# A graph network with soft and routed experts on one core: earlier expert weights, a token list made on chip, more logit tiles and smaller pieces of work in the edge stage

## The chip, the cores and the metric

The kernel runs on one core of a Trainium2 chip. Its engines are TensorE (PE; PEld is the loading of its weights), VectorE (DVE), ScalarE (ACT), GpSimd (POOL) and SyncE (SP, which issues transfers); ACT and POOL issue transfers too. Each engine works through its own instructions in order and waits at semaphores for the others. The metric is the time of one execution on the device in microseconds, the median of several.

## The reference

The input is x (1250 rows of 768 numbers) and 40000 edges from a source row to a destination row, sorted by destination. Four blocks follow each other, each of the form x = x + f(layernorm(x)):

```
# 1. two layers of graph attention (8 heads of 96, then 1 head of 768); in each:
fs, fd = x @ Ws + bs, x @ Wd + bd
e      = leaky_relu(fs[src] + fd[dst], 0.2)
logit  = (e * attn).sum(per head)                  # one per edge
alpha  = softmax of logit over the edges with the same dst
out    = elu(sum over those edges of alpha * fs[src])      # then a layer norm with weights
# 2. soft experts: 32 experts with 32 slots each (1024 slots), hidden width 192
logits = l2norm(x) @ (scale * l2norm(phi))
slots  = softmax(logits over an expert's slots).T @ l2norm(x)
eo     = gelu(slots @ w1[e] + b1[e]) @ w2[e] + b2[e]
out    = softmax(logits over all 1024 slots) @ eo
# 3. two graph convolutions with self-loops and symmetric normalization
# 4. routed experts: 8 experts, hidden width 1152, the top 2 of 8 for each row
out    = sum of gate * (gelu(x @ w1[e] + b1[e]) @ w2[e] + b2[e])
```

## The kernel before

The 1250 rows are ten blocks of 128 partitions (NB = 10; the last has 98 rows). The edges are sorted on the chip into 100 buckets (NBK), by block of the destination (i) and block of the source (j), k = 10 i + j; a bucket has up to 512 edges (CAP), four columns of 128. The stages run one after the other, each fed by the one before. Four of them bear on the change.

**The second edge stage** (`edge_logits`, L361 to L585; heads = 1) makes one logit for each edge. For every bucket k of a loop, and every column q, PE sums the source's and the destination's features by products with one-hot matrices into `z` (L425; each operand in a high and a low half, 8 matmuls for a column), DVE takes the positive part times the attention vector and adds it up into column q of the tile `lg` (L440), and ACT copies the linear part (L447). Two buckets' worth of steps later DVE adds the linear part (L458), and POOL scatters each column, 128 single numbers, into a table in DRAM, one entry for each pair of rows (L463). `done` holds the newest bucket first, and q's scatter belongs to `done[1 + 2 q]`: column 0 of a bucket is scattered two iterations after its sums, column 3 eight iterations after. `lg` has 12 buffers in this stage and 8 in the first edge stage. A second use of the same loop, with heads = 8, is the first edge stage.

At the end of the loop (k = 99, 100 and 101) `dense.join` (L707; its addition is L714) adds the two halves of the linear features of five, four and one of the ten blocks into `rows`. Three pairs of tables (`lt`, logits, and `ct`, edge counts) for the blocks 0 to 2 are loaded during the loop.

**The second dense stage** (`run_alone`, L774) takes one destination block at a time, in an order that is written out for PE, DVE, ACT and POOL. `maxima` is the negated maximum of a block's logits, `exponentials` its exp (L798), `turn` transposes the exp on PE (L807) and multiplies it by the counts on DVE (L808), `product` multiplies by the features (L813). Each product of block b is followed by a generator `ending` (L1130), of which `go_on` runs one step at each call, two calls for each block: elu, layer norm, the row sum on POOL (L1148 to L1150), the second norm and the squares (ACT), until `xn` holds the normalized rows. Its remaining steps run in the soft stage's loop, with the same `go_on`. `phi_norm` normalizes phi between the products. `neg`, a helper of elu and the square's output, has one buffer, g has three; the layer norm's weights `lw`, `lb` are loaded into tiles of their own at the start, and `phi` too, in SP's queue.

**The soft experts** (L1267 to L1342): the slots' inputs `slT` are a product over all rows (L1267). Then eight groups of four experts. `first_layer(g)` loads four w1 (on SP's queue) and four w2 (on ACT's), 576 KB each, with eight buffers each, multiplies (L1298; b1 is added by a product at the start) and applies gelu (ACT, L1301). `second_layer` follows with w2, and `combine` with the 1250 rows (L1327); the sum of group g runs after the second layer of g+1. The pool `route`, with xn and g, is closed after `slT`; then the pool `experts` opens, with weights and b1, b2. The order of instructions among engines is made by the framework's planner here.

**The second graph convolution and the routing** (`convolution_by_counts`, the loop from L1576 on): for each block PE runs two halves of 20 products (L1583). In between, in an order written out for PE, DVE and ACT, stand the routing steps of the blocks before: `normalize`, `turn` (transpose), `logits`, `choose` (DVE: softmax, the best two of eight, gates), `rank` (PE: how many rows of this block precede each row at its expert), `places` (DVE: the position in the expert's list; POOL scatters (row, gate) to the position in `slots_d`, in DRAM, L1476), `bias` (PE: the gates times b2, L1486; DVE adds it, L1487; SP writes the row to the output). Three more iterations finish the last three blocks. Then DVE plans the 27 blocks of the expert stage from the counts (L1688 to L1724), and `fetch(i)` reads 128 entries of `slots_d` and gathers their rows of `xl_d` (L1733) with POOL. In the expert stage each of these blocks runs a first and a second product (L1758, L1768).

## Time and profile before

| | us |
|---|---|
| median of three runs | 3940.41 (3930.57 to 3949.85) |
| the profiled execution, its time | 3940.67 |
| the profiled execution, its span | 3939.0 |
| PE busy | 3640.9 |
| DVE busy | 2305.5 |
| POOL busy | 1523.5 |
| ACT busy | 1207.0 |
| mean granted clock of TensorE | 0.964 of full speed |

The stages that bear on the change lie in the span so: second edge stage to 2276, second dense stage to 2462, soft logits to 2588, slot inputs to 2688, soft experts to 2906, second convolution with routing from 3153 to 3275, its last three blocks and the plan to 3320, expert blocks to 3939.

In a line of a group, "out<-in" are the program's names of tiles, "xcount" is the number of instructions, and times are microseconds. "DVE c L440 <- DMA logit<-lg,where: 41.2, 17, 6.1" reads: before its instructions of line 440, DVE waited 41.2 us in 17 waits for those transfers, 6.1 at the longest. In a chain of work each line is a start, a length and what ran, and "issue" is time in which the engine waited for nothing that the profile shows.

### The profile page before, as it was taken

The page shows a single profiled execution, that of the slowest core. Times are in us where ns is not written, and L with a number is a line of the kernel's source. Part 1 is how long each engine was busy: PE and PEld are TensorE (multiplying, and loading weights), DVE is VectorE, ACT ScalarE, POOL GpSimd, SP SyncE. Part 2 cuts the span into 40 slices and gives each one's busy share as a digit, 9 for nine tenths or more (in the row PEclk, how much of TensorE's full clock was granted, in tenths as well). Part 3 has the DMA queues.
Part 4 walks back from the last instruction along what each step waited for, and adds up shares of the span by engine and source line. Part 5 has one row for each costly group of instructions (what it writes and reads, how often), then busy time and mean ns, then how long its engine had stood idle before and what let it go on. Part 6 is the DMA issues. An engine that isn't in the chain of part 4 may idle for free.

```text
span 3939.0 us, 52779 instructions
## 1 busy us (share of the span) xinstructions
PE 3640.9 (92%) x19239; PEld 2845.4 (72%) x19239; DVE 2305.5 (59%) x4071; ACT 1207.0 (31%) x3932; POOL 1523.5 (39%) x1369
## 2 busy tenths in 40 slices
PE   6999799999978889899999979996999997999999
PEld 3444699999978886589999945442457686777776
DVE  7887799999988882277777758620552153000000
ACT  1111366666667882122222223310011121111110
POOL 2555388888872332246666743100001011111111
PEclk9999899999989999999999989997999997999999
DMA  9920222311225441245555350007721025788888
GB/s 344 328 85 17 93 57 81 91 51 54 56 68 215 180 155 57 91 84 57 66 71 50 41 107 24 0 0 197 189 90 33 0 82 190 285 325 328 314 325 293
DMA packets 314333, 509.48 MB, mean 129 GB/s; under 512 B 55310, under 2 KB 193134, under 8 KB 314060
## 3 DMA queue, kind: packets, MB, share of 16 engines
q1 hardware_dynamic: 268062, 450.40, 37.9%
q10 hardware_dynamic: 13774, 35.38, 3.0%
q0 software_dynamic: 32224, 20.20, 2.3%
q8 instruction: 154, 2.52, 0.3%
q14 instruction: 119, 0.97, 0.1%
HBM read 407.05 MB, written 100.96 MB: 129 GB/s over the span
## 4 chain that ended last, share of the span: by engine, by line
PE 48%; DMA 9%; DVE 8%; issue 4%; POOL 2%; ACT 2%; SPq 0%; DVEq 0%; POOLq 0%; ACTq 0%
PE bank L1758 8%; PE acc L1768 7%; DMA logit<-lg,where 6%; PE z L425 5%; PE bank L1003 4%; PE acc L185 4%; PE acc L1327 3%; PE acc L1211 3%; PE acc L1267 2%; PE acc L1583 2%; POOL logit L463 2%; PE bank L1567 2%; PE po L858 2%; PE po L813 2%; DMA w<-in_L_ffn_w_dram 1%
## 5 line engine op out<-in xcount | busy, mean ns | idle before, releaser
L463 POOL DMA_INDIRECT logit<-lg,where x780 | 810.1, 1039 | 362.6 <-issue 190.5
L440 DVE SCALAR_TENSOR_TENSOR c<-z,a 128x768 f32<-128x768 f32 x680 | 640.2, 950 | 142.1 <-PE z L425 92.4
L425 PE MATMUL z<-rows,oh 128*128 128x392 f32 (+4 forms) x1560 | 551.1, 353 | 49.2 <-ACT lin L447 29.3
L425 PE MATMUL z<-sl,oh 128*128 128x392 f32 (+4 forms) x1560 | 537.9, 345 | 0.9 <-DVE sl L394 0.9
L425 PE MATMUL z<-dl,oh 128*128 128x392 f32 (+5 forms) x1560 | 536.8, 344 | 0.0
L425 PE MATMUL z<-dh,oh 128*128 128x392 f32 (+5 forms) x1560 | 536.7, 344 | 0.0
L1771 DVE TENSOR_SCALAR y<-acc,sl 128x768 f32<-128x768 f32 x25 | 25.4, 1018 | 557.4 <-PE acc L1768 557.4
L425 PEld LDWEIGHTS z<-rows,oh 128*128 128x128 f32 (+1 forms) x1560 | 300.2, 192 | 59.3 <-ACT lin L447 37.4
L1758 PEld LDWEIGHTS bank<-xT,w 128*128 128x128 f32 x2700 | 305.2, 193 | 10.4 <-issue 9.8
L1758 PE MATMUL bank<-xT,w 128*128 128x128 f32 x2700 | 308.6, 277 | 0.4 <-ACT xT L85 0.4
L425 PEld LDWEIGHTS z<-sl,oh 128*128 128x128 f32 (+1 forms) x1560 | 300.5, 193 | 1.5 <-DVE sl L394 1.5
L425 PEld LDWEIGHTS z<-dl,oh 128*128 128x128 f32 (+1 forms) x1560 | 298.4, 191 | 0.0
L1768 PE MATMUL acc<-w,hT 128*128 128x384 f32 x900 | 298.2, 487 | 0.0
L425 PEld LDWEIGHTS z<-dh,oh 128*128 128x128 f32 (+1 forms) x1560 | 298.0, 191 | 0.0
L450 DVE TENSOR_REDUCE lg<-c 128x8 f32<-128x768 f32 x290 | 275.7, 951 | 6.5
L1768 PEld LDWEIGHTS acc<-w,hT 128*128 128x128 f32 x900 | 167.6, 191 | 106.2
L405 DVE TENSOR_SCALAR oh<-idx,own 128x1024 fp32r<-128x1024 bf16 x200 | 226.2, 1131 | 1.2 <-DMA fd_d<-y 1.2
L455 ACT ACTIVATE c<-c 128x96 f32<-128x96 f32 x800 | 224.0, 301 | 0.0
L895 ACT ACTIVATE ex<-lt,top 128x1280 f32<-128x1280 f32 (+1 forms) x80 | 213.4, 2670 | 24.1 <-PE bank L928 22.3
L435 POOL TENSOR_TENSOR c<-c,a 128x768 f32<-128x768 f32 x100 | 186.7, 1867 | 56.4 <-ACT lin L445 41.9
L447 ACT COPY lin<-z 128x1 f32<-128x1 f32 x390 | 62.1, 159 | 470.7 <-DVE c L440 469.0
L858 PE MATMUL po<-rows,aT 128*128 128x97 f32 (+1 forms) x1600 | 197.3, 282 | 2.3 <-DVE aT L934 2.3
(348 smaller groups left out, 6097.2 us busy)
## 6 DMA issues: line engine op xcount, KB each, us to landing
w<-in_L_ffn_w_dram SPq DMA_DIRECT2D x51, 3456.0 KB
logit<-none SPq DMA_DIRECT2D x100, 512.0 KB
idx<-idx_d SPq DMA_DIRECT2D x200, 256.0 KB
lt<-logit SPq DMA_DIRECT2D x90, 512.0 KB
w<-in_L_ffn_w_dram SPq DMA_DIRECT2D x32, 576.0 KB
w<-in_L_ffn_w_dram ACTq DMA_DIRECT2D x32, 576.0 KB
logit<-lg,where POOLq DMA_INDIRECT x780, 4.3
ct<-pairs_d SPq DMA_DIRECT2D x18, 576.0 KB
```

Source lines behind the costliest of these rows:

```text
L185: nc.tensor.matmul(p[:n, h, :HF], xT[:, k, b * P:b * P + n], w[:, k, h * HF:(h + 1) * HF], start=(k == 0), stop=(row is None and k == KD - 1))
L405: nc.vector.tensor_scalar(oh, idx.rearrange("p (a c) -> p a c", a=2), own, None, op0=ALU.is_equal)
L425: nc.tensor.matmul(o, self.oh[:n, a, q * P:(q + 1) * P], rows[b, w][part][:n, h * HW:h * HW + widths[h]], start=(a == 0 and part == "h"), ...
L435: nc.gpsimd.tensor_mul(c, c, attn)
L440: nc.vector.scalar_tensor_tensor(alone(c, heads), self.features(q), 0.0, alone(attn, heads), op0=ALU.max, op1=ALU.mult, **more)
L450: nc.vector.tensor_reduce(self.lg[:, q, :], self.c[q].rearrange("p (h d) -> p h d", h=heads), AX.X, ALU.add)
L455: nc.scalar.activation(x, x, AF.Copy, accum_out=self.lg[:, q, h:h + 1])
L463: nc.gpsimd.indirect_dma_start(out=table[self.k][:, :], out_offset=bass.IndirectOffsetOnAxis(ap=where[:, q, self.k:self.k + 1], axis=0), i ...
L858: nc.tensor.matmul(po[:n, h // 4, c:c + hd + 1], aT[:, s, :n], fs[s][:, f:f + hd + 1], start=(s == 0), stop=(s == NB - 1))
L895: nc.scalar.activation(x[:n], self.loaded[b][0][:n, :, h], AF.Exp, bias=self.tops[b][:n, h:h + 1])
L1758: nc.tensor.matmul(pt[:, c - c0, :], w1[:, k, c * P:(c + 1) * P], xT[:, k, :], start=(k == 0), stop=(k == KD - 1))
L1768: nc.tensor.matmul(p[:, h, :HF], hT[:, c, :], w2[:, c, h * HF:(h + 1) * HF], start=(c == 0), stop=(c == KH - 1))
```

## The change

In the second edge stage `lg` has 24 buffers rather than 12 (the first keeps 8). A block's terms are joined one per iteration from k = 91 to k = 100, and the negated maximum of block 0 is taken at k = 100 by the new method `maximum`; `run_alone` takes the others.

In the endings `xn`, g, `neg`, `lw` and `lb` are parts of five shared tiles, `xa`, `xb`, `xc` (three, three and four blocks of xn), `ga` (three g) and `gb` (neg, lw, lb). The scale is loaded before lw and lb. A `yield` stands between the normalization and the square, so an ending has one step more. `pr` takes the buffer of `sq`.

In the soft experts the pool `route` stays open, and the weights take its tiles: the w1 of even groups in `ga` and `gb`, of odd groups in `xa` and `xb`; the first two w2 of a group in a new tile `gc` or in `xc`, the others in `w2b`, two buffers in the pool `experts`. The four w1 and two w2 of group 0 are issued before the slots' inputs. b1 is added by the last product of a group.

In the routing, each block gets `first_places`: its positions, a one-hot matrix `hot` of the positions in expert 0's list, and a column of gates in `valued`, beside the row's number. A sum of products `hot` by `valued` (`first_hots`) gives the first list of 128 rows and gates, and `first_rows` gathers the rows from it; `fetch(0)` returns these. `choose` loses a memset (except in the last block), a copy and one addition. The transposed rows of two blocks lie in halves of one tile `space`. The end of the loop is written out by itself: the last iteration leaves out rank, logits and bias, the last three blocks follow step by step, and the biases of blocks 7, 8 and 9 come after the plan. The same is done in the other form of the convolution, which these inputs don't use.

```diff
 self.sides, self.z, self.c = [], {}, {}
-self.lg = dense.even.tile([P, CAP // P, heads], F32, name="lg", bufs=4 + 4 * apart)
+self.lg = dense.even.tile([P, CAP // P, heads], F32, name="lg", bufs=8 if first else 24)
 self.lin = ep.tile([P, CAP // P, heads], F32, name="lin", bufs=3)
...
     done[1 + apart * q].scatter(q)
-for j in {NBK - 1: range(NB // 2), NBK: range(NB // 2, NB - 1), NBK + 1: (NB - 1,)}.get(k, ()):
-    dense.join(split["sh"][j], split["sl"][j])
+if first:
+    ended = {NBK - 1: range(NB // 2), NBK: range(NB // 2, NB - 1), NBK + 1: (NB - 1,)}.get(k, ())
+else:
+    ended = (k - 1 - (NB - 1) * NB,) if k > (NB - 1) * NB else ()
+for j in ended:
+    if j < NB:
+        dense.join(split["sh"][j], split["sl"][j])
+if not first and k == NBK:
+    dense.maximum(0, dense.even)
 done = [b] + done[:-1]
...
+def maximum(self, b, pool):
+    n = ROWS[b]
+    self.tops[b] = top = pool.tile([P, 1], F32, name="top", bufs=3)
+    nc.vector.tensor_reduce(top[:n, :], self.loaded[b][0][:n].rearrange("p s h -> p h s"), AX.X, ALU.max)
+    nc.vector.tensor_scalar_mul(top[:n, :], top[:n, :], -1.0)
...
 nc.sync.dma_start(phi, t["L0_ffn_phi"].rearrange("(k p) e s -> p k (e s)", p=P))
-lw = bcast(t["L0_gnn_lno_w"], D, rp, "low")
-lb = bcast(t["L0_gnn_lno_b"], D, rp, "lob")
 scale = rp.tile([P, 1], F32, name="scale")
...
                                  ap=[[0, P], [1, 1]]))
-xn = rp.tile([P, NB, D], F32, name="xn")
+parts = {x: rp.tile([P, n, D], F32, name=x) for x, n in (("xa", 3), ("xb", 3), ("xc", 4), ("ga", 3), ("gb", 3))}
+lw, lb = parts["gb"][:, 1, :], parts["gb"][:, 2, :]
+for y, x in ((lw, t["L0_gnn_lno_w"]), (lb, t["L0_gnn_lno_b"])):
+    nc.sync.dma_start(y, bass.AP(tensor=x.tensor, offset=x.offset, ap=[[0, P], [1, D]]))
+def xn_of(b):
+    return parts[("xa", "xb", "xc")[min(b // 3, 2)]][:, b - 3 * min(b // 3, 2), :]
...
 mv = rp.tile([P, 2], F32, name="mv", bufs=6)
-g = rp.tile([P, D], F32, name="g", bufs=3)
-neg = rp.tile([P, D], F32, name="neg")
+g = parts["ga"][:, b % 3, :]
+neg = parts["gb"][:, 0, :]
 nc.sync.dma_start(x[:n], t["x"][b * P:b * P + n, :])
...
 yield
-y, ss = xn[:n, b, :], rp.tile([P, 1], F32, name="ss", bufs=3)
+y, ss = xn_of(b)[:n], rp.tile([P, 1], F32, name="ss", bufs=3)
 normalize(y, x[:n], mv, n)
-neg = rp.tile([P, D], F32, name="neg")
+yield
 nc.scalar.activation(neg[:n], y, AF.Square, accum_out=ss[:n])
...
+HH = HID // 2
+def weights(g, w2b):
+    tags = ("xa", "xb", "xc") if g % 2 else ("ga", "gb", "gc")
+    w1, w2 = [], []
+    for i in range(2):
+        x = rp.tile([P, 2, KD, HID], F32, name="w1", tag=tags[i])
+        y = rp.tile([HH, 2, 2, D], F32, name="w2", tag=tags[2]) if i == 0 else w2b
+        for q in range(2):
+            e = 4 * g + 2 * i + q
+            if x is not None:
+                nc.sync.dma_start(x[:, q], t["L0_ffn_w1"][e].rearrange("(k p) h -> p k h", p=P))
+            if y is not None:
+                nc.scalar.dma_start(y[:, q], t["L0_ffn_w2"][e].rearrange("(j p) d -> p j d", p=HH))
+            w1.append(x[:, q])
+            w2.append(y[:, q] if y is not None else None)
+    return w1, w2
+early = weights(0, None)
 slT = xp.tile([P, KD, ES], F32, name="slT", tag="phi")
...
-route.close()
 with tc.tile_pool(name="experts", bufs=1, reuse_waits="tile") as xp:
-    HH = HID // 2
     b1 = xp.tile([NE, HID], F32, name="b1")
...
 def first_layer(g):
-    w1, w2 = [], []
-    for q in range(4):
-        e = 4 * g + q
-        w = xp.tile([P, KD, HID], F32, name="w1", bufs=8)
-        nc.sync.dma_start(w, t["L0_ffn_w1"][e].rearrange("(k p) h -> p k h", p=P))
-        w1.append(w)
-        w = xp.tile([HH, 2, D], F32, name="w2", bufs=8)
-        nc.scalar.dma_start(w, t["L0_ffn_w2"][e].rearrange("(j p) d -> p j d", p=HH))
-        w2.append(w)
+    w2b = xp.tile([HH, 2, 2, D], F32, name="w2b", bufs=2)
+    if g == 0:
+        w1, w2 = early
+        for q in range(2, 4):
+            w2[q] = w2b[:, q - 2]
+            nc.scalar.dma_start(w2[q], t["L0_ffn_w2"][q].rearrange("(j p) d -> p j d", p=HH))
+    else:
+        w1, w2 = weights(g, w2b)
     whose = owner[:, 4 * g:4 * g + 4, :].rearrange("e q s -> e (q s)")
     ph = bank().rearrange("p a b -> p (a b)")
-    nc.tensor.matmul(ph[:, :HID], whose, b1, start=True, stop=False)
     for k in range(KD):
...
         nc.tensor.matmul(ph[q * SLOTS:(q + 1) * SLOTS, :HID], slT[:, k, c0:c0 + SLOTS], w1[q][:, k, :],
-                         start=False, stop=(k == KD - 1))
+                         start=(k == 0), stop=False)
+nc.tensor.matmul(ph[:, :HID], whose, b1, start=False, stop=True)
 hh = xp.tile([P, HID], F32, name="hh", bufs=2)
...
 def turn(self):
-    pool, tag = self.space
-    self.xT = pool.tile([P, KD, P], F32, name="xT", tag=tag)
+    self.xT = self.space[:, :, self.b % 2 * P:(self.b % 2 + 1) * P]
     transposed(self.xT, self.xl, self.n)
...
 nc.scalar.activation(prob[:n], pt[:n, 0, :MOE], AF.Exp, bias=v[:n], accum_out=total[:n])
-nc.vector.memset(self.both, 0.0)
+if n < P:
+    nc.vector.memset(self.both, 0.0)
 nc.vector.reciprocal(total[:n], total[:n])
 nc.vector.tensor_scalar(prob[:n], prob[:n], total[:n], None, op0=ALU.mult)
-nc.vector.tensor_copy(left[:n], prob[:n])
 self.entry = entry = rt.tile([P, 2, 2], I32, name="entry", bufs=4)
...
 v = self.column("v")
-nc.vector.tensor_reduce(v[:n], left[:n], AX.X, ALU.max)
-nc.vector.scalar_tensor_tensor(pick[:n], left[:n], v[:n], order[:n], op0=ALU.is_equal, op1=ALU.mult)
+of = left if i else prob
+nc.vector.tensor_reduce(v[:n], of[:n], AX.X, ALU.max)
+nc.vector.scalar_tensor_tensor(pick[:n], of[:n], v[:n], order[:n], op0=ALU.is_equal, op1=ALU.mult)
 nc.vector.tensor_reduce(v[:n], pick[:n], AX.X, ALU.max)
...
     if i == 0:
-        nc.vector.scalar_tensor_tensor(left[:n], pick[:n], -2.0, left[:n], op0=ALU.mult, op1=ALU.add)
+        nc.vector.scalar_tensor_tensor(left[:n], pick[:n], -2.0, prob[:n], op0=ALU.mult, op1=ALU.add)
     nc.vector.scalar_tensor_tensor(x[:n], pick[:n], 1.0, prob[:n], op0=ALU.mult, op1=ALU.mult,
                                    accum_out=entry[:n, i, 1:2].bitcast(F32))
-    nc.vector.tensor_add(self.both[:n], self.both[:n], pick[:n])
     self.picks.append(pick)
+nc.vector.tensor_add(self.both[:n], self.picks[0][:n], self.picks[1][:n])
 nc.vector.tensor_mul(self.gates[:n], self.both[:n], prob[:n])
...
+def first_places(self, on):
+    n, pc, b = self.n, self.pc, self.b
+    self.pos = self.by_expert("pos")
+    nc.vector.tensor_add(self.pos, place, pc[:, 0, :MOE])
+    nc.vector.tensor_add(place, place, pc[:, 1, :MOE])
+    self.hot = self.space[:, b // 2, (2 + b % 2) * P:(3 + b % 2) * P]
+    on.tensor_scalar(self.hot[:n], self.space[:n, KD - 1, 2 * P:3 * P], self.pos[:n, 0:1], self.both[:n, 0:1],
+                     op0=ALU.is_equal, op1=ALU.mult)
+    on.tensor_copy(valued[:n, b, 1:2], self.gates[:n, 0:1])
...
 n, pc = self.n, self.pc
-pos, x = self.by_expert("pos"), self.by_expert("x")
-nc.vector.tensor_add(pos, place, pc[:, 0, :MOE])
-nc.vector.tensor_add(place, place, pc[:, 1, :MOE])
-self.gT = rt.tile([MOE, P], F32, name="gT")
+x = self.by_expert("x")
+self.gT = rt.tile([MOE, P], F32, name="gT", tag=("gT", "b1r", "slots")[self.b % 3])
 nc.vector.tensor_copy(self.gT[:, :n], pc[:MOE, 2, :n])
...
 to = rt.tile([P, 1], I32, name="to", bufs=4)
-nc.vector.scalar_tensor_tensor(x[:n], self.picks[i][:n], 1.0, pos[:n], op0=ALU.mult, op1=ALU.mult,
+nc.vector.scalar_tensor_tensor(x[:n], self.picks[i][:n], 1.0, self.pos[:n], op0=ALU.mult, op1=ALU.mult,
                                accum_out=v[:n])
...
+def counted(space):
+    nc.gpsimd.iota(space[:, KD - 1, 2 * P:3 * P], pattern=[[1, P]], base=0, channel_multiplier=0,
+                   allow_small_or_imprecise_dtypes=True)
+    return space
+def first_hots(rows_p, blocks):
+    for x in blocks:
+        nc.tensor.matmul(rows_p[:, 0, :2], x.hot[:x.n], valued[:x.n, x.b, :], start=(x.b == 0), stop=(x.b == NB - 1))
+def first_rows(rows_p):
+    f = rt.tile([P, 1], F32, name="v", bufs=2)
+    sl = rt.tile([P, 2], F32, name="mv1", bufs=2).bitcast(I32)
+    nc.vector.tensor_scalar_add(f, rows_p[:, 0, 0:1], float(N))
+    nc.vector.tensor_copy(sl[:, 0:1], f)
+    nc.vector.tensor_copy(sl[:, 1:2].bitcast(F32), rows_p[:, 0, 1:2])
+    xs = rt.tile([P, D], F32, name="xl", bufs=2)
+    nc.gpsimd.indirect_dma_start(
+        out=xs, out_offset=None, in_=xl_d[:, :], in_offset=bass.IndirectOffsetOnAxis(ap=sl[:, 0:1], axis=0))
+    return sl, xs
...
-    for b in range(NB + 3):
-        live = b < NB
+    for b in range(NB):
+        last = b == NB - 1
         one, two, three = routed
         one.normalize()
-        if live:
-            p = acc()
-            half(b, p, 0)
-        two.choose()
-        one.turn()
-        if live:
-            half(b, p, 1)
-        two.rank()
-        one.logits()
-        if not live:
+        p = acc()
+        half(b, p, 0)
+        if last:
+            one.turn()
+            two.choose()
+        else:
+            two.choose()
+            one.turn()
+        half(b, p, 1)
+        n = ROWS[b]
+        if not last:
+            two.rank()
+            one.logits()
+            three.bias()
+        nc.vector.scalar_tensor_tensor(halves(xk[:n, b, :]), p[:n, :, :HF], scale[:n, b:b + 1],
+                                       halves(xk[:n, b, :]), op0=ALU.mult, op1=ALU.add)
+        if not last:
+            two.first_places(nc.gpsimd)
             two.places()
-        three.bias()
-        if live:
-            n = ROWS[b]
-            nc.vector.scalar_tensor_tensor(halves(xk[:n, b, :]), p[:n, :, :HF], scale[:n, b:b + 1],
-                                           halves(xk[:n, b, :]), op0=ALU.mult, op1=ALU.add)
-            two.places()
-        routed = [Routed(b, gp, "w", "slots") if live else Nothing(), one, two]
-return first
+            if b >= 2:
+                all_routed.append(two)
+        routed = [Routed(b, space, "slots"), one, two]
+    end, one, two = routed
+    two.rank()
+    one.logits()
+    end.normalize()
+    two.first_places(nc.vector)
+    two.places()
+    rows_p = acc()
+    first_hots(rows_p, all_routed)
+    end.turn()
+    one.choose()
+    end.logits()
+    one.rank()
+    first_hots(rows_p, [two])
+    end.choose()
+    one.first_places(nc.vector)
+    end.rank()
+    first_hots(rows_p, [one])
+    end.first_places(nc.vector)
+    first_hots(rows_p, [end])
+    rows = first_rows(rows_p)
+    one.places()
+    end.places()
+    three.bias()
+return first, rows, (two, one, end)
...
 nc.vector.tensor_copy(row_i, f)
+for x in late:
+    x.bias()
...
 def fetch(i):
+    if i == 0:
+        return first_list
```

## The prediction

> **What bounds the kernel now.** I read the page's totals first, then a table of stages, then, stage by stage, the waits and the chain.
>
> ```profile
> PE 3640.9 (92%) x19239; PEld 2845.4 (72%) x19239; DVE 2305.5 (59%) x4071; ACT 1207.0 (31%) x3932; POOL 1523.5 (39%) x1369
> ```
>
> TensorE is busy 92% of 3939.0 us; some 300 us are left in which it isn't, so the table must say where these lie. Columns: stretch, its length, then busy time of PE, PEld, DVE, ACT, POOL, the granted clock, the DMA share, GB/s.
>
> ```profile
> 1741.00:2276.00 535.00, 508.06 (x2800) 502.00 (x2800) 399.74 (x898) 118.44 (x543) 356.09 (x353) 0.98 0.51 56
> 2588.00:2688.00 100.00, 98.13 (x232) 43.34 (x231) 6.53 (x9) 3.04 (x3) 0.00 (x0) 1.00 0.01 2
> 2688.00:2755.00 67.00, 36.53 (x281) 15.84 (x280) 2.78 (x4) 3.87 (x6) 0.00 (x0) 0.64 1.09 278
> 3275.00:3320.00 45.00, 16.69 (x51) 10.43 (x52) 20.88 (x106) 3.63 (x9) 11.57 (x16) 0.50 0.58 208
> 3320.00:3939.00 619.00, 610.15 (x3743) 486.56 (x3741) 39.86 (x49) 75.53 (x250) 79.77 (x73) 0.99 0.85 310
> ```
>
> In order: second edge stage (PE idle 27 us), slot inputs (PE full, DMA empty), start of the soft experts (PE idle 30, DMA full), routing tail (idle 28), expert blocks (PE-bound; the change leaves their work alone). Who is waited for in the second edge stage (total, times, longest):
>
> ```profile
> DVE c L440 <- PE z L425: 72.8, 114, 4.5
> DVE c L440 <- DMA logit<-lg,where: 41.2, 17, 6.1
> PEld z L425 <- ACT lin L447: 30.9, 19, 4.2
> PE z L425 <- ACT lin L447: 24.7, 17, 3.9
> ```
>
> DVE waits for scatters (its logit tile is not free), ACT for DVE, PE for ACT: one stall, counted three times. The chain at the end of this stage:
>
> ```profile
> 2275.67 0.74 DVE rows L714
> 2276.41 12.21 issue
> 2288.63 0.36 ACT L798
> ...
> 2291.34 2.59 PE bank L807 x10
> ```
>
> Between the last edge sum and the dense stage's first transposes lie 15.8 us, mostly joins on DVE. The chain at the start of the soft experts:
>
> ```profile
> 2687.51 18.95 DMA w<-in_L_ffn_w_dram
> ...
> 2711.47 23.55 DMA w<-in_L_ffn_w_dram
> ...
> 2735.59 14.15 DMA w<-in_L_ffn_w_dram
> ```
>
> 56.65 us of waiting for weights. In the routing tail:
>
> ```profile
> 3287.74 2.78 PE acc L1486 x4
> ...
> 3303.20 3.35 DMA slots_d<-entry,to
> ...
> 3309.79 7.46 DMA xs<-xl_d,sl
> 3317.29 1.56 PE bank L166 x6
> ```
>
> The first list goes to DRAM and back before its rows can be fetched.
>
> **A, second edge stage.** The sum starts from the profiled run, 3940.67 us (span 3939.0; the median, 3940.41, is the same to 0.01%). With 24 logit tiles instead of 12, bucket k needs the scatters of bucket k-24, so DVE's 41.2 us of waits go as long as POOL is under 16 buckets late. PE alone: its longest unbroken piece has 392 matmuls in 69.43 us, 0.177 each, 1.417 for the eight of one c; the 353 c's from 1741 on need 500 us and end at 2241. Taking away only PE's own 24.7 us of waits gives 2251. DVE is late next: per bucket 4 c's of 0.88 and some 0.8 for the rest is 4.35 against PE's 5.6, so not before the last row. There a bucket has three columns (PE 4.2) and now a join too (0.97): DVE 4.5, 0.3 more than PE, some 3 us over ten buckets. After the last sum one join, the maximum already taken, ACT's table load and one exp are left: some 7.5 us for 15.8. So the dense stage starts between 2241 + 7.5 = 2248 and 2251 + 3 + 7.5 = 2261 instead of 2291.3: 30 to 43 us.
>
> Not all stays. POOL's scatters are no faster: 371 from 1741 to 2320 take 377.7 us and 196.3 us of idle, 93.8 of it waiting for earlier scatters to land. The last starts at 2314 and, with at most the 10.5 us of its waits for DVE gone, at 2303 to 2312. POOL runs in order: the three ops that end block 0 (1.82, 2.05 and 1.93 us, at 2329.7 in the trace) stand behind these scatters, and DVE's statistics of block 0, some 57.5 us after the dense start, behind those. With a start at 2248 they are due at 2305, so scatters ending at 2312 hold DVE, then PE, by 12.5 us. Also phi and the layer-norm rows now load beside the last scatters, and stretch their landings. Value: -33, between -20 (30 less 10) and -44.
>
> Joins among scatters: the eight scatters beside the ten joins took 1.399 us against 1.018, together 3.0 us. The kernel before paid that too, so I add nothing. The GPSIMD Engine Reference of the Trainium skill (section 1, Specifications) says that POOL shares its memory interface with VectorE, with contention when a DVE instruction has two inputs there; that speaks against the move. By it a join could hold POOL for its whole 0.97 us, 9.7 us for ten, an estimate, three times the row.
>
> **B, second dense stage's endings.** The row is ACT's `neg` waiting for DVE's g: 56.9 us, six times, longest 12.1. Squares get a step of their own, and the last scaling (1.79 us on DVE, behind the wait for the square) moves to the next call. But PE is busy 157.8 of 171.0 us here, and what it waits for is in other rows (phi's squares, exponentials, transposes' evacuations), so ACT's wait is covered by PE's products. Uncovered, the extra step delays only the last block: about one call's DVE work, 4 us. The order of SP's loads changes (scale before the two rows), the bytes don't. Value 0, -4 to +4.
>
> **C, soft experts.** Six loads of 576 KB (3.54 MB) move ahead of the slot inputs, where the DMA share is 0.01: four on SP's queue, two on ACT's. SP and ACT have nothing to issue there except ACT's evacuations, so issuing costs nothing. At 278 GB/s 3.54 MB are 12.7 us: that is the least gain if transfers alone set the pace. The most is PE's whole idle time to the steady state, 30.5 us in this stretch, and some 5 us of clock (0.64: 46 first-layer products took 4.49 us after a wait, 22 took 1.10 once warm; three groups). Group by group: first(0) no longer waits and runs at 2686 to 2688. What follows is 2 w2 of group 0, then group 1: odd groups' tiles are freed only by the end of the slot inputs (2685), so their w1 and w2 begin where group 0's began before: first(1) at about 2703, when 4 w1 have landed (the fourth did at 2704.8), first(2) about 2715, first(3) about 2727; its products then run unbroken from about 2730 instead of 2755.4. ACT's queue also gains: w2 of group 1 stood behind gelu(0), which ended at 2710.6 and now ends near 2689. From there on groups are PE-bound (148.5 of 151 us), with 4.7 MB per 21.5 us, 219 GB/s of 278. The bias product at the end of the accumulation instead of its start is the same instruction. Value -28, -12 to -36.
>
> **D, routing.** In the loop, first_places adds two POOL ops per block (a 128x128 compare and a column). No POOL row is like it; 128x768 ones take 1.8 to 2.05, a 128x2 iota 0.125, so 0.1 to 2 us, nearest a sixth of the large one, 0.4. POOL is busy 14.4 of 122 us there, which hides it; uncovered it would delay the slot scatters behind it, which nothing reads before the tail. Ten products of 128x2 on PE at 0.2 to 0.45 (the rows of rank) are 2 to 4.5 us, most of them in PE's idle time of the tail.
>
> The tail: the last half ends at 3271.4. Before, rank, logits and bias of block 6, then normalizing, two choices and a cold bias (2.78) lead to the last choice at 3296, the places and the plan to 3301.5, then the scatter of slots (0.95+3.35), their reload (about 3.2 with its issue), the gather (7.46): rows at 3317.3. After: block 6's bias (1.41 warm, and 0.95 + 0.95 of DVE behind it) and block 7's (2.78 and 0.86) leave the path, 4 to 6 us; block 9's last choice ends near 3285; rank 1.2, three DVE ops of the one-hot 0.8, the product 0.5 and three small DVE ops 0.6 give the list at about 3288. The gather, 6 to 7.5 us, lands at 3295. The plan no longer stands before it, nor do slot scatter and reload. But four biases now lie between: cold, 4 x 2.8 = 11.2 us, to about 3299. The first expert product then starts at 3299 to 3301 instead of 3319.25: -19. Least: the second expert's weights, 3456 KB at about 400 GB/s, are issued at 3301 and needed at about 3313, a stall of up to 5 us, and the next list's rows come about then: -12. Most: biases beside the gather, -24.
>
> Of TensorE's clock, the trace shows 0.50 in this tail, one bias at 1.41 warm and 2.78 cold, and 14.17 us for the first 108 expert products against some 12.1 later. TensorE: Matmul & The Clock Gate in the Trainium skill (Part 1) says that the clock is halved when idle and freed after about 3.4 us of sustained work. By that the four biases would take 3.4 + 3.9 = 7.3 us, 3.9 less than by the row, an estimate. I keep the row.
>
> **Sum**: -33 + 0 - 28 - 19 = -80, so 3861 us. By the extremes: -108 (3833) and -40 (3901).
>
> **Rivals.**
> 1. POOL stays the bound of A. For it: POOL's idle time is its own transfers' (93.8 us), DVE's part of it 10.5. Against: nothing of the dense stage but POOL's endings waits for the last rows. If statistics wait for scatters that end at 2314 and are stretched by the loads, A gives -12: 3882.
> 2. The soft experts stay bound by transfers, as the order of PE is left to the planner, which may put first(1) ahead of work that is ready. For it: share 1.09 and 278 GB/s in the stretch. C gives -12: 3877.
> 3. Slower: shared tiles bring false waits. `neg` and the layer-norm rows lie in one tile now, the three g's in another, xn in three; if a write waits for every reader of its tile, each block's ACT `neg` stands behind POOL's three ops of the block before, 5.8 us, up to the longest such wait already seen, 12.1. Over nine blocks that is 52 to 109 us: 3913 to 3970. It cancels the gain at 8.9 us per block. Against: xn is one tile already, written by DVE for one block while others are read, and no wait of this kind stands in the rows.
>
> **How the numbers follow.** The forecast 0.55, its own range 3833 to 3901; rival 1 0.15; rival 2 0.12; rival 3 0.18, half of it past +0.5%, 0.05 between. 0.5% (20 us) is about what a measurement can tell from no change. Faster: 0.55 + 0.15 + 0.12 + 0.04 = 0.86; same 0.05; slower 0.09. From 3830 to 3915 all is held but most of rival 3 and a few hundredths below.
>
> **What the profile will show.** A: no waits of DVE for scatters past start-up, dense transposes by 2261; wrong if these remain, or POOL's g ops wait while DVE stands. B: `neg` waits fall, PE's idle time doesn't. C: DMA share over 0.3 in the slot inputs, unbroken products some 25 us earlier relative to their end. D: no reload of slots before the first gather, first expert product within 30 us of the last half instead of 48. The prediction is wrong if waits at L1148 to L1166 grow by more than 6 us per block, or if the expert blocks' 24.4 us change.

## The result and the profile after

The changed kernel takes 3889.17 us (median of 3885.67 to 3898.57) against 3939.44 us (median of four runs, 3930.57 to 3949.85); its ratio to the kernel before is 0.988, 95% interval 0.9861 to 0.990. That is 50 us less, where 80 were forecast: the sign and the place were right, the size was not. The profiled execution took 3888.52 us, its span is 3886.9.

Times of the same events in the two profiles, read from the instructions of each line (us from the start of the span):

| | before | after | change since the row above |
|---|---|---|---|
| first edge product of the second edge stage | 1670.0 | 1668.1 | -1.9 |
| last edge product | 2273.0 | 2234.7 | -36.4 |
| first transposes of the second dense stage | 2291.3 | 2245.8 | -7.1 |
| last product of the dense stage | 2459.4 | 2438.7 | +24.8 |
| first soft logits | 2462.7 | 2443.4 | +1.4 |
| end of the slots' inputs | 2685.4 | 2666.0 | -0.1 |
| last sum of the soft experts | 2903.7 | 2868.0 | -16.2 |
| last half of the second convolution | 3271.5 | 3234.6 | -1.3 |
| first product of the expert blocks | 3319.2 | 3266.4 | -15.9 |
| last product | 3930.2 | 3877.9 | +0.6 |

Three stages gained, as forecast, and one lost: the dense stage, from 168.0 to 192.8 us. The stages of the changed kernel in the table of stretches (PE, PEld, DVE, ACT, POOL busy, clock, DMA share, GB/s):

```profile
1741.00:2236.00 495.00, 493.39 (x2798) 492.75 (x2796) 411.43 (x907) 117.66 (x539) 321.95 (x318) 1.00 0.55 60
2246.00:2439.00 193.00, 160.78 (x529) 93.84 (x530) 111.94 (x212) 55.11 (x71) 91.15 (x70) 0.90 0.36 69
2666.00:2720.00 54.00, 35.82 (x285) 15.69 (x285) 3.56 (x5) 5.04 (x8) 0.00 (x0) 0.72 1.09 276
3234.00:3266.00 32.00, 25.12 (x95) 18.12 (x93) 21.46 (x118) 3.31 (x8) 7.86 (x11) 0.57 0.54 170
3266.00:3878.00 612.00, 610.25 (x3744) 486.78 (x3744) 40.66 (x57) 76.75 (x251) 80.07 (x76) 1.00 0.86 319
```

PE is now busy 493 of 495 us in the edge stage: DVE's waits for scatters are gone from its rows. In the dense stage PE stands for 32 us. What DVE waits for there, and the chain through the longest of these waits:

```profile
DVE st L1139 <- POOL xk L1167: 29.1, 1, 29.1
```

```profile
2312.58 8.50 DMA logit<-lg,where
...
2326.88 0.97 POOL logit L463
2327.84 0.03 issue
2327.87 1.81 POOL ga L1165
2329.68 1.76 POOL xk L1166
2331.44 0.07 issue
2331.51 1.81 POOL xk L1167
2333.32 0.02 issue
2333.34 1.03 DVE st L1139 x2
```

This is one queue: POOL finishes its last scatter of the edge stage at 2327.8 and only then makes the three operations that end block 0 (a multiplication and two additions; "the additions" below). DVE reached the statistics of that sum at 2304.2 and stands until 2333.3. Behind them in DVE's order come the counts times block 4's transposes (L820), and PE waits for these, 24.3 us at the longest, where the kernel before shows 3.1:

```profile
PE bank L819 <- DVE aT L820: 28.6, 9, 24.3
```

At the start of the soft experts and in the tail:

```profile
PE bank L1331 <- DMA w<-in_L_ffn_w_dram: 18.2, 5, 8.6
```

```profile
3238.64 3.08 PE acc L1545 x14
...
3253.34 0.59 PE acc L1545 x2
3253.93 10.55 PE acc L1532 x16
3264.50 0.95 DVE xk L1533
```

PE's waits for weights fell from 30.5 to 18.2 us and did not vanish. In the tail the products of the one-hot matrices (L1545) lie in the chain, and the four biases (L1532) stand between them and the expert blocks.

### The profile page after: what moved, and what is told of

Read it like the earlier page. It is cut to its first block, busy times and chain, and to the rows that moved or that the text cites. A ratio compares the mean times of both kernels' runs of the same rounds, so it can differ in the third digit from the quotient of the medians.

```text
span 3886.9 us, 52772 instructions
## 1 busy us (share of the span) xinstructions
PE 3628.1 (93%) x19259; PEld 2836.4 (73%) x19259; DVE 2307.0 (59%) x4051; ACT 1206.9 (31%) x3932; POOL 1528.3 (39%) x1384
## 4 chain that ended last, share of the span: by engine, by line
PE 54%; DVE 7%; DMA 4%; issue 4%; ACT 2%; POOL 1%; SPq 1%; POOLq 0%; DVEq 0%; ACTq 0%
PE z L425 12%; PE acc L1876 7%; PE bank L1866 7%; PE acc L185 4%; PE bank L1015 4%; PE acc L1361 3%; PE acc L1228 3%; PE acc L1304 2%; DMA logit<-lg,where 2%; PE acc L1653 2%; PE bank L1636 2%; PE po L825 1%; DVE c L440 1%; PE po L870 1%; PE bank L166 1%
## 5 line engine op out<-in xcount | busy, mean ns | idle before, releaser
L425 PE MATMUL z<-rows,oh 128*128 128x392 f32 (+4 forms) x1560 | 545.9, 350 | 26.1 <-DVE oh L405 14.2
```

The source lines that it names most:

```text
L425: nc.tensor.matmul(o, self.oh[:n, a, q * P:(q + 1) * P], rows[b, w][part][:n, h * HW:h * HW + widths[h]], start=(a == 0 and part == "h"), ...
```

## The experiments

Theory one: what the dense stage lost is POOL's order of work, the start of the soft experts is paced by transfers, the tail by biases and the gather. The rivals were the loads beside the last scatters, the tiles' whole gain, PE's work, and the gather alone.

**First set, another chip.** In this set the kernel before took 4016.67 us, and the edge products of the changed kernel's variants ended 60 to 110 us later than on the other chips. The four kernels therefore say little on the edge stage, but the stages after it ran as on the first chip.

The additions that end blocks 0 and 1 on DVE:

```diff
-                nc.gpsimd.tensor_mul(g[:n], g[:n], lw[:n])
-                nc.gpsimd.tensor_add(x[:n], x[:n], lb[:n])
-                nc.gpsimd.tensor_add(x[:n], x[:n], g[:n])
+                adds = nc.vector if b < 2 else nc.gpsimd
+                adds.tensor_mul(g[:n], g[:n], lw[:n])
+                adds.tensor_add(x[:n], x[:n], lb[:n])
+                adds.tensor_add(x[:n], x[:n], g[:n])
```

> The changed kernel with the three additions that end blocks 0 and 1 of the second dense stage put on DVE instead of POOL. Theory one (POOL's order: DVE stood 29.1 us before the statistics of block 0 because POOL's additions are queued behind scatters that end at 2327.8): the 29.1 us wait goes, DVE pays 6 additions of about 1 us, the dense stage takes 168 to 175 us instead of 192.8, the whole 3865 to 3872 instead of 3889. Theory two (the loads beside it, phi and logits, set the pace of this stage): another wait of 15 us or more takes its place and the whole stays above 3880.

12 logit tiles:

```diff
-                    self.lg = dense.even.tile([P, CAP // P, heads], F32, name="lg", bufs=8 if first else 24)
+                    self.lg = dense.even.tile([P, CAP // P, heads], F32, name="lg", bufs=8 if first else 12)
```

> The changed kernel with 12 logit tiles again in the second edge stage; joins and the first maximum stay in the loop. Theory one (the end of the scatters sets when the dense stage can go on, whatever the number of tiles): the edge products end near 2268 instead of 2234.7, the dense stage starts near 2279, DVE's 29 us wait for POOL shrinks to under 5 us, and the dense stage's products end 8 to 15 us later than 2438.7; the whole 3897 to 3905. Theory two (the tiles' whole 33 us reach the end): 3915 to 3925.

The two early w2 of group 0 on SP's queue:

```diff
-                                nc.scalar.dma_start(y[:, q], t["L0_ffn_w2"][e].rearrange("(j p) d -> p j d", p=HH))
+                                (nc.scalar if g else nc.sync).dma_start(y[:, q], t["L0_ffn_w2"][e].rearrange("(j p) d -> p j d", p=HH))
```

> The changed kernel with the two early w2 loads of group 0 on SP's queue behind the four w1, not on ACT's, where they ran at 2238 to 2263, beside phi and the last scatters. Theory one (loads stretch the scatters' landings): 1.18 MB of the 5.0 MB that were loaded there leave, the last scatter starts 3 to 8 us earlier than 2326.9, DVE's 29.1 us wait falls by as much, the whole 3881 to 3886. Theory two (POOL's scatters have a pace of their own): last scatter and wait within 2 us of before, the whole at 3889.

The soft experts' weights as before:

```diff
-                early = weights(0, None)
...
+            route.close()
...
-                    if g == 0:
-                        w1, w2 = early
...
+                    for q in range(4):
+                        e = 4 * g + q
+                        w = xp.tile([P, KD, HID], F32, name="w1", bufs=8)
...
+                    nc.tensor.matmul(ph[:, :HID], whose, b1, start=True, stop=False)
```

> The changed kernel with the soft experts' weights of the kernel before (own tiles, all loads after the slots' inputs, b1 first). Theory one (transfers set the pace at the start of the soft experts, so six early loads of 576 KB are worth their 12.8 us at 276 GB/s and little more): soft experts 216 to 220 us instead of 202.1, and, as no w2 runs beside the last scatters, 3 to 8 us less waiting in the dense stage; the whole 3897 to 3903. Theory two (the forecast's 28 us from PE's unbroken products): 227 us or more, the whole 3910 or more.

| | ratio to before | last edge product | dense stage | last scatter's end after the first transposes | soft experts | tail |
|---|---|---|---|---|---|---|
| additions on DVE | 0.9881 (0.9846 to 0.9917) | 2349.1 | 166.2 | 32.6 | 200.6 | 31.9 |
| 12 tiles | 0.9889 (0.9863 to 0.9915) | 2333.5 | 166.3 | 32.5 | 201.1 | 31.9 |
| w2 on SP | 0.9891 (0.9865 to 0.9916) | 2325.6 | 166.3 | 30.9 | 200.5 | 31.3 |
| weights not early | 0.9919 (0.9892 to 0.9946) | 2333.5 | 166.0 | 32.6 | 218.0 | 31.3 |

The expected times of the first three could not be tested: with the edge products so late, scatters end 31 to 33 us after the dense stage's first transposes, long before DVE needs block 0's sum, and no stall is left that an edit could take away. That is itself evidence: the dense stage takes 166 us with 24 tiles and POOL's additions unchanged (the third kernel) when the scatters end in time. The fourth decides its question: the early weights are worth 17.2 us (218.0 less the 200.7 that its neighbours take in the mean). That is within theory one's 216 to 220, and far from the 28 us of the forecast.

**Second set**, on a chip where the kernel before takes 3939.86 us: both kernels unedited, the additions on DVE and the 12 tiles again.

> The changed kernel, unedited, beside the next three on one chip. In the runs so far beside the kernel before on another chip, edge products ran to 2326 to 2349 and the dense stage took 166.0 to 166.3 us, since the last scatter started only 31 to 33 us after its first transposes; in the changed kernel's first profile this was 81 us and the stage took 192.8. Theory one (POOL's order): the dense stage takes 166 us plus what the last scatter's distance from the first transposes exceeds by 53 us. Theory two (loads): 185 us or more, whatever this distance.

> The kernel before, unedited, with a profile on the chip of its neighbours. Theory one: edge products end 8 us or more after those of the changed kernel where the scatters wait for landings, and not later at all where the events of the stage itself are late; dense stage 166 to 168, soft experts 218, tail 47 to 48.

> The changed kernel with the three additions that end blocks 0 and 1 of the second dense stage on DVE, again, beside the changed kernel. Theory one (POOL's order): where the changed kernel's dense stage takes over 185 us, this takes 168 to 175 and the whole is 18 to 25 us shorter; where that one takes 166, this too, within 3 us. Theory two (loads): the dense stage as long as the changed kernel's, within 5 us.

> The changed kernel with 12 logit tiles, again, beside the changed kernel. Theory one: edge products end 20 to 35 us later than with 24, the dense stage has no wait of DVE for POOL over 5 us, and its products end 8 to 15 us later; where the edge products of both end after 2320, no difference beyond 10 us. Theory two (the tiles' whole gain reaches the end): dense products end 25 us or more later.

| | ratio to before | last edge product | first transposes | scatters end | last dense product | dense stage |
|---|---|---|---|---|---|---|
| before | 1.0003 (0.9989 to 1.0017) | 2268.4 | 2288.1 | 2308.9 | 2455.7 | 167.7 |
| changed | 0.9865 (0.9831 to 0.990) | 2231.4 | 2242.7 | 2324.6 | 2434.3 | 191.7 |
| additions on DVE | 0.9805 (0.977 to 0.984) | 2236.2 | 2247.5 | 2322.3 | 2418.5 | 171.1 |
| 12 tiles | 0.9894 (0.9858 to 0.993) | 2275.1 | 2287.7 | 2321.5 | 2453.1 | 165.4 |

DVE's waits in the dense stage of the changed kernel:

```profile
DVE st L1139 <- POOL xk L1167: 28.1, 1, 28.1
DVE aT L820 <- PE bank L819: 19.1, 8, 7.1
DVE top L734 <- DMA lt<-logit: 16.2, 3, 9.7
```

and with the additions on DVE:

```profile
DVE aT L820 <- PE bank L819: 24.8, 9, 7.4
DVE top L734 <- DMA lt<-logit: 13.8, 2, 12.2
DVE mv L1153 <- PE po L825: 9.1, 4, 4.2
```

Theory one's numbers hold: in the changed kernel the last scatter starts 81 us after the first transposes, which by its rule makes 194 us for the 191.7 measured, and the kernel before shows its 167.7 (and a tail of 48.0 us, as expected; its soft experts take 216.2 us where 218 was expected). Six operations moved to another engine take 20.6 us off the dense stage, and the kernel goes from 3886.98 to 3866.92 us. The scatters end hardly earlier (2322.3 against 2324.6) and the edit leaves the loads as they are, so what cost the time is the place of these operations in POOL's order, behind the scatters. One of them, the multiplication of 128x768, takes 0.958 us on DVE and 1.814 on POOL:

```profile
L1166 POOL TENSOR_TENSOR ga<-ga,gb x6: 1808/1814/1818, 2330.5 to 2409.5; 128x768 f32<-128x768 f32 x6
L1166 DVE TENSOR_TENSOR ga<-ga,gb x2: 958/958/959, 2293.7 to 2310.8; 128x768 f32<-128x768 f32 x2
```

With 12 tiles the edge products end 43.7 us later, more than the 20 to 35 expected; no row of DVE waits for POOL, the dense stage falls to 165.4, and its end is 18.8 us later, between the two theories' numbers (8 to 15, and 25 or more). So of 44 us that the tiles free, 19 reach the end and 25 come back in the dense stage, where DVE waits 28.1 us for POOL.

**Third set**, on a chip where the kernel before takes 3941.1 us. Additions on DVE and the early w2 on SP's queue together:

> The changed kernel with the additions of blocks 0 and 1 on DVE, and the two early w2 loads on SP's queue behind the four w1, so that they leave the stretch of the last scatters. With the additions alone the dense stage took 171.1 us, with one wait of DVE for block 3's logits of 12.2 us left. Theory one (the loads at the start of the dense stage, phi 3.15 MB, two rows 0.8, w2 1.2, stand before these logits): with w2 away the wait falls to 6 to 9 us, the dense stage to 166 to 169; 2 to 5 us under the additions alone, ratio to before 0.979 to 0.980. Theory two (the logits wait for their scatters): wait and stage within 2 us.

The same, and phi's load between the products of block 0, with SP's order written out:

```diff
-            nc.sync.dma_start(phi, t["L0_ffn_phi"].rearrange("(k p) e s -> p k (e s)", p=P))
...
+                if step == 0:
+                    nc.sync.dma_start(phi, t["L0_ffn_phi"].rearrange("(k p) e s -> p k (e s)", p=P))
...
-                                                 mybir.EngineType.Activation, mybir.EngineType.Pool}):
+                                                 mybir.EngineType.Activation, mybir.EngineType.Pool, mybir.EngineType.SP}):
```

> As the last, and phi is loaded between the products of block 0, behind block 3's logits in SP's queue, SP's order written out in the dense stage. Theory one: no wait of DVE for logits over 2 us, the dense stage 164 to 168 us, unless the squares of phi come late and PE waits for them instead. Theory two: the wait stays, dense stage 171.

Only four loads ahead, and no extra step in the ending. A one-element copy from the slots' inputs holds the two w2 back. Since square and elu share one `neg`, the square here overwrites it before elu's sum has read it, so other values are computed; only the times are read.

```diff
                 normalize(y, x[:n], mv, n)
-                yield
                 nc.scalar.activation(neg[:n], y, AF.Square, accum_out=ss[:n])
...
+                        w2a = rp.tile([HH, 2, 2, D], F32, name="w2", tag="gc")
+                        for q in range(2):
+                            nc.scalar.copy(w2a[0:1, q, 0, 0:1], slT[0:1, KD - 1, ES - 1:ES])
```

> The changed kernel with the additions of blocks 0 and 1 on DVE, only the four w1 of group 0 ahead of the slots' inputs, the two w2 held until their end, and the ending without the extra step ahead of the square. Transfers: two loads of 576 KB less ahead should cost 1.18 MB at 276 GB/s, 4.3 us, if transfers set the pace of the soft experts' start (soft experts from the end of the slots' inputs 203 to 206 us instead of 200 to 202), and nothing if the first layers' w1 alone set it. Extra step: by the forecast worth 0 within 4 us from the dense stage's start to the end of the soft logits (290.5 us with the additions on DVE, of which up to 5 us for w2 that is no longer loaded there); if ACT's wait had cost PE time, 10 us or more longer.

The late biases left out:

```diff
             for x in late:
-                x.bias()
+                nc.sync.dma_start(out[x.b * P:x.b * P + x.n, :], xk[:x.n, x.b, :])
```

> The changed kernel without the products that add b2 for the rows of blocks 7, 8 and 9 (their rows are written without this term). Theory one (the first gather, issued at 3254.6, lands at 3261 to 3262 and bounds the tail just behind the biases): the first expert product 29 to 30 us after the last half instead of 31.8, the whole 1 to 3 us shorter. Theory two (the four biases set the start, the rows were there long before): 24 us, the whole 7 us shorter.

| | us | ratio to before | dense stage | first transposes to end of soft logits | soft experts | tail |
|---|---|---|---|---|---|---|
| additions on DVE, w2 on SP | 3861.01 | 0.9799 (0.9774 to 0.9824) | 165.7 | 289.0 | 197.2 | 31.4 |
| and phi later | 3877.48 | 0.9842 (0.9815 to 0.9869) | 185.1 | 307.6 | 200.0 | 31.4 |
| four loads, no extra step | 3870.67 | 0.9824 (0.9795 to 0.9852) | 168.5 | 287.7 | 203.3 | 31.5 |
| late biases left out | 3878.23 | 0.9849 (0.9815 to 0.9883) | 192.4 | 314.8 | 202.2 | 26.1 |

The first row has the lowest time found, 26 us under the changed kernel's 3886.98 in the second set (on chips where the kernel before takes 3941.1 and 3939.86 us). As a whole it can't be told from the additions alone (0.9799 against 0.9805, with overlapping intervals). In its dense stage theory one holds and more: DVE's wait for block 3's logits, 12.2 us with the additions alone and expected at 6 to 9, is gone from its rows, and the stage is at the 166 us that it takes without a stall. The two w2 did not leave the stretch of the last scatters, as was expected of them: they were issued at 2293 to 2300, behind those logits in SP's queue, where ACT's queue had issued them at 2238.2. The scatters ended at 2331.1, no earlier.

Phi behind the logits too is worse: the logits come in time, and phi does not.

```profile
ACT sq L1196 <- PE pn L1198: 36.3, 3, 19.9
ACT sq L1196 <- DMA phi<-in_L_ffn_phi_dram: 20.2, 1, 20.2
PEld pn L1198 <- ACT sq L1196: 17.2, 4, 10.4
PE pn L1198 <- ACT sq L1196: 13.4, 4, 9.8
```

The squares of phi wait 20.2 us on ACT, and PE behind them. That was the condition named in its expectation.

The third row: the stretch to the end of the soft logits is 287.7 us without the extra step and with no w2 loaded in it, 289.0 in the first row, which has both, and 288.7 to 289.9 in the first set. So step and loads together cost 1 to 2 us, and ACT's 56.9 us of waiting before cost PE nothing that shows.

With four early loads the soft experts take 203.3 us, just inside the 203 to 206 that were named for transfers, and 1 us more than the longest of the ten profiles with six (197.2 to 202.3). But this length moves with the granted clock, so PE's idle time says more. The whole stage with four early loads, and with six in the first row (columns as in the table of stretches):

```profile
2643.40:2846.70 203.30, 186.16 (x1025) 86.58 (x1024) 85.84 (x92) 12.79 (x21) 0.00 (x0) 0.91 0.67 168
2639.00:2836.20 197.20, 177.57 (x1025) 83.48 (x1024) 85.81 (x92) 12.61 (x19) 0.00 (x0) 0.95 0.66 168
```

PE is idle 17.1 us with four early loads, 15.6 to 19.9 in the ten profiles with six, and 31.0 to 34.4 in the three with none. In the two of the ten that ran at the same clock of 0.91 it is 15.6 and 16.0, so the two w2 ahead are worth at most some 1.5 us and not the 4.3 of transfers. What parts 197.2 from 203.3 is PE's busy time, 177.6 against 186.2 us, at a clock of 0.95 against 0.91. PE's waits at the first layer in the kernels with six early loads (second set), four, and none (first set):

```profile
PE bank L1331 <- DMA w<-in_L_ffn_w_dram: 17.1, 5, 8.1
```

```profile
PE bank L1334 <- DMA w<-in_L_ffn_w_dram: 16.9, 5, 7.4
```

```profile
PE bank L1316 <- DMA w<-in_L_ffn_w_dram: 32.1, 8, 9.6
PE bank L1312 <- DMA b<-in_L_ffn_b_dram: 2.0, 1, 2.0
```

Over all profiles these waits for w are 15.4 to 19.7 us with six early loads, 16.9 with four, and 28.5 to 32.1 with none. The four w1 take some 13 us off them, the two w2 little or nothing; the wait for b1, 1.8 to 2.1 us, is gone as well. Bytes over bandwidth (12.8 us for six loads) came near the result, but not as the transfers' sum: what counts is the w1.

The fourth row: without three biases the tail is 5.7 us shorter, between its two theories (2 to 3, and 8). PE then waits for the rows themselves:

```profile
PE bank L166 <- DMA xl<-xl_d,mv: 2.0, 1, 2.0
```

The rows were there 24.2 us after the last half (transposes at 3257.8, the half's end at 3233.6), 3.2 us after the gather's instruction had ended. So in the changed kernel they lie ready and the biases hold the expert blocks back by 5.7 us.

## Why the prediction was right in sign and too large in size

**A.** DVE's waits for scatters went, PE ran unbroken and the dense stage began at 2245.8, where 2248 to 2261 was forecast: 45.5 us earlier, even more than the 30 to 43. The step that failed is the term for what comes back. Its mechanism was right, and so was its time: statistics due at 2305, reached at 2304.2. But the scatters were to end at 2303 to 2312 and the wait to be at most 12.5 us; they ended at 2327.8, and the wait was 29.1 us. The forecast took POOL's timeline of before and subtracted up to 10.5 us of POOL's waits for DVE's edge sums. These did not go; before and after:

```profile
POOL logit L463 <- DVE c L440: 10.5, 19, 3.3
```

```profile
POOL logit L463 <- DVE c L440: 15.6, 18, 9.0
```

In the changed kernels of the second and third set, with 12 tiles as with 24, the last scatter starts 631 to 645 us after the first; in the two profiles of before it is 617 and 625. The 22 us by which the changed kernel is longer in the second set lie in two rows of POOL's waits: those for landings are 100.1 us against 87.2, those for DVE's edge sums 13.3 against 4.9. In the first pair of profiles, 14 us apart, the landings hardly differ (95.3 against 93.8). Why these waits grew was not settled: the scatters fall farther behind both in the middle of the stage and among the dense stage's loads; moving w2 or phi within that stretch did not shorten it. The ten joins among the scatters are not it: twelve scatters beside them take 1.34 us against 1.00, together 4 us, where the joins of before cost 3. Rival 1 had the scatters end at 2314 or later and A at -12; on both it was nearer than the forecast, though that the loads stretched the scatters, as it had it, was not shown. From the first row of the table to the soft logits A and B gave 17.4 us, 19.3 with the earlier start, where -33 was forecast, just outside A's bounds of -20 to -44.

**B.** Zero was forecast, and the run without the extra step shows 1.3 us, the loads of w2 included. The `neg` wait went as named, but ACT now waits elsewhere: 55.1 us for DVE's statistics (L1162), a wait that is 46.5 us in the kernel whose dense stage takes 165.7 us, so it costs PE nothing that shows either. The shared tiles of rival 3 brought no wait: the only row of this kind in the changed kernel is

```profile
ACT gb L1157 <- DVE gb L1156: 6.0, 3, 5.0
```

and it was there before, on `neg`, with 5.8 us.

**C.** The failed term is the -28: it was read off the moment from which PE's products run unbroken. That moment did move: PE's last wait for a weight ends 64.4 us after the slots' inputs in the kernel before (at 2749.8; the forecast had read 2755.4) and 38.3 us after them in the changed one (at 2704.3). But up to it the old kernel had done 12 us more work (32.1 us busy against 20.1). The saving is PE's idle time in the stage, 32.5 us before (218.3 less 185.9 busy) and 18.4 after (202.1 less 183.7). With 2.2 us of busy time, at a granted clock of 0.92 instead of 0.89, it makes 16.2 us, in the bounds of -12 to -36 and near the -12 that transfers alone, or rival 2, would give.

The order that rival 2 named, a group's first layer ahead of work that is ready, does show. Group 0's second layer has its input (hT) at 2675.4, but its first products (L1351) stand on PE behind a first-layer product of group 1 (L1331), which waits 8.65 us for its weight:

```profile
2674.94 0.42 DVE L1343 COPY hT<-bank 96x256 f32<-96x256 f32 x1 [8.26 <-PE bank L1341]
2686.63 0.53 PE L1331 MATMUL bank<-w,slT 128*32 128x192 f32 x1 [8.65 <-DMA w<-in_L_ffn_w_dram]
2686.64 0.85 PE L1351 MATMUL acc<-w,hT 96*32 96x384 f32 x1
```

The rows give these products no wait for their own weights, the last of which was issued at 2666.9. No run changed this order, so how much of the 18.4 us of idle time it costs stays open.

The weights for group 1 began at 2660.0, 6 us before the slots' inputs ended, as their first tile was free by then; the forecast had them begin at that end. The DMA share over 0.3 in the slots' inputs that was named as a sign did not show (it was 0.05): the six early loads had run before, two w2 from 2238.2, two w1 from 2458.2 and two from 2486.9.

**D.** -15.9 us in the tail for the forecast's -19; the first expert product came 31.8 us after the last half, where at most 30 was named. The list took longer: the gather was issued 20.0 us after the last half (3254.6 less 3234.6) where the list was forecast after 16.6. The products of `hot` by `valued` for the blocks 0 to 6 (14 instructions, 3.08 us) lie in the chain, and the forecast had put them into PE's idle time. The four biases cost 10.55 us for the forecast's 11.2, by the cold row. The gather was priced too high (6 to 7.5 us from the list; 3.2 after its instruction in the run that left the late biases out), which cost nothing, since the biases end later.

The row also decides the question on the clock. By the Trainium skill, TensorE: Matmul & The Clock Gate (Part 1), the clock is freed after some 3.4 us of sustained work, which made 7.3 us for the four biases an estimate. The biases kept PE busy for 10.50 of 10.50 us in the stretch from 3253.9 to 3264.4, at a granted clock of 0.50 throughout:

```profile
3253.90:3264.40 10.50, 10.50 (x18) 4.88 (x17) 6.05 (x34) 0.00 (x0) 4.86 (x5) 0.50 0.41 145
```

Here the measurement differs from the page and decides. The clock was 0.50 until 3269.2, 2.8 us after the first expert product, and 1.00 from then on.

The sum: -19.3 (A, B), -16.2 (C), -1.3 in the convolutions before the last half, -15.9 (D), +0.5 for the rest, so -52 in the profiles' spans. A, C and D all came out towards the small end of their bounds, and so the time lies near the slow end of the range of 3833 to 3901. The expert blocks took 611.5 us against 610.9, unchanged as forecast.

## What to carry to other kernels

When a wait is removed, follow every engine's queue past the place where it stood: here POOL's scatters ended at 2324.6 instead of 2308.9, and 25 of 44 us came back in a stage that waited for three operations queued behind them; giving these operations of the first two blocks, six in all, to DVE, which stood waiting for them, brought 20 us. A gain read off "when the work runs unbroken" counts work that is only shifted; count idle time of the bounding engine over the whole stage, which also sets aside what the clock gives or takes. A load that is moved ahead is worth what its first reader waits for it: the four w1 loads took some 13 us off PE's waits, the two w2 beside them little or nothing.

## What the runs showed of the hardware that was not expected

On the chip of the first set the second edge stage took 60 to 110 us longer than on the others; the stages after it took as long as there. In its profiles a part of ACT's waits there is put down to nothing that the profile shows, and some of DVE's to "remote"; with 12 tiles, and with the additions on DVE:

```profile
ACT lin L447 <- issue: 145.1, 81, 4.9
DVE c L440 <- remote: 22.4, 9, 4.7
```

```profile
DVE c L440 <- PE z L425: 131.3, 85, 4.8
DVE c L440 <- remote: 51.1, 9, 9.0
```

On the chip of the second set the row of ACT's waits for nothing visible has 0.5 us in the changed kernel. The cause stays open; no run was made to find it. The ratio to the kernel before was much the same there (0.988 to 0.989 for the changed kernel's variants with early weights), though the stage that was changed most ran otherwise.
